# All four elements of a group turned by the DMA engines, in two halves through one free tile

## The chip, the cores and the metric

The kernel runs on one core of a Trainium2 chip. The metric is the device time of one execution in microseconds (us). Before the change the median of two runs is 2303.45 us (2301.77 and 2305.13).

The core's engines work side by side, each through its own list of instructions in order: TensorE (PE: matmuls; PEld: loading the stationary operand), VectorE (DVE), ScalarE (ACT), GpSimd (POOL) and SyncE (SP), which in this kernel issues every DMA. An instruction that must wait holds up all that stands behind it on its engine. That holds for SP too: a DMA that waits for its source holds up the DMAs listed after it.

## The reference

The input `x` holds 128 elements of 128 nodes with 512 features each, in float32. Two layers follow one another; each normalises, applies a graph operation and adds the result to its input:

```python
h = jnp.maximum(_layernorm(x, axis=-1), 0.0)
x = x + norm_adj @ (h @ W0) + b0            # layer 0, for each element
h = jnp.maximum(_layernorm(x, axis=-1), 0.0)
q, k, v = h @ Wq + bq, h @ Wk + bk, h @ Wv + bv      # 8 heads of 64
attn = softmax(q @ k.T / 8 + (1 - adj) * -1e9)
x = x + (attn @ v) @ Wo + bo                # layer 1, for each element
```

The change touches `h` of layer 1. The products with Wq, Wk and Wv contract over the features, so `h` has to lie with features on the partitions, while the normalisation leaves it with nodes on the partitions. Each 128x128 block must be transposed.

## The kernel before, in words

**Groups and blocks.** The 128 elements are worked in 32 groups of four (`GB = 4`, `NG = 32`); the elements of a group are b = 0 to 3, and b = 0, 1 are its first half, b = 2, 3 its second. An iteration t has five blocks of seven steps: W (layer 0's weight product of group t+1), Q, K and V (projections of group t), and Y (attention's output product of group t-1). Each of these products of 512 by 512 is a two-level Winograd scheme of seven products, which is why operands have extra slots of sums and differences (`combine`, lines 359 to 370). The last two parts of a block's last product are put into steps 1 and 2 of the next block (the list `tail`): TensorE writes `bank_c`, VectorE adds it to its target, and then `bank_c` is written again.

**The order.** The order of all instructions is written out by hand. `at(t, place, f, ...)` puts a function in front of a step of TensorE's dense work: "Y2" is in front of step 2 of block Y, "Y0b" after its matmuls and before its later reads. `block` (line 1012) calls them in that order, and each engine keeps to it.

**What belongs to the transposition of `h`.** In iteration t, group g = t+1 is prepared. For groups 2 to 30:

- `norm_h` (ScalarE, line 333) writes `h` of b = 0 and 1 at V1 and V2, and of b = 2 and 3 at V5 and V6.
- `split_h` (line 677) at V2b and V3: a 32-bit element is two 16-bit halves. ScalarE copies `h` of b = 0 and then b = 1 into a tile of two planes (line 682), all first halves in one plane and all second halves in the other. The tile is `att_of(g - 1, -1)`, the one attention tile of five that is free then. After the second copy SP stores the tile into `planes_h` in DRAM (line 684).
- `turn_h` (line 686) at Y0: a DMA transpose reads `planes_h` and writes eight slots of the operand tile `op_norm` (line 689).
- `transpose_h` (line 667) for b = 2 and 3 at Y1 and Y2: four TensorE transposes against the identity into a PSUM bank (line 674), and a ScalarE copy from there into `op_norm` (line 675).
- `attention_operands` (line 691) at Y5: GpSimd makes the sums and differences (lines 362 to 365 and 90), which block Q of iteration t+1 uses.

Groups 0, 1 and 31 are transposed by TensorE alone. The free tile is used again in the same iteration by `split_att` of b = 0 at Y3b (line 787): ScalarE writes the planes of the attention there, and SP stores them (line 791).

**SP's list around it.** From V3 on: the store of `planes_h` (line 684), a part of a weight reload (line 992), the DMA transpose of Y0 (line 689), weight parts at Y0, Y1 and Y3 (line 992), the store of `planes` at Y3b (line 791), a weight part at Y5, the store of a half result (line 834), two weight parts at W0, another store of `planes` at W1b, the store of the other half and the load of the first half of x of group t+2 at W3 (lines 834 and 161), the last weight part, the load of the second half at W5, and then the attention's transposes (line 794) between stores and weight parts.

**The use of x.** When x of group t+2 has landed, VectorE takes its statistics for layer 0 (line 314, first half at Q0b). On VectorE these stand between the reads of block W's tail (line 429).

Of the kernel before, what the change touches and what calls it, by code (L numbers as in the profile page):

```python
# [9 lines left out]
U16 = mybir.dt.uint16  # L10
# [16 lines left out]
A11, A12, S1, A22, S2, S3, S4 = range(7)  # L27
# [17 lines left out]
LEFT_AT = {A11: 0, A12: 4, S1: 8, A22: 12, S2: 16, S3: 20, S4: 24}  # L45
# [48 lines left out]
def kernel(  # L94
# [16 lines left out]
    nc = tc.nc  # L111
    B, N, D = x.shape
    P = 128
    H = 8
    HD = D // H
    NC = D // P
# [6 lines left out]
    dp = ctx.enter_context(tc.tile_pool(name="dp", bufs=1, space=bass.MemoryType.DRAM))  # L123
# [22 lines left out]


    planes_dram = [dp.tile([P, 2, H * P], U16, tag=f"planes_{b}", name=f"planes_{b}") for b in range(GB)]
    h_dram = dp.tile([P, 2, H * P], U16, tag="planes_h", name="planes_h")
    adj_sb, an = (att_buf[2][:, i, :] for i in range(2))  # L150
    bias_part = att_buf[4][:, 0:NC, :].rearrange("p c f -> p (c f)")
    ones = att_buf[4][:, NC, :]
# [220 lines left out]
    op_mix, op_norm, op_att = (Operands(f"op_{k}") for k in "aho")  # L373
# [303 lines left out]
    def split_h(g, b):  # L677


        h2 = hs.pop((g, b)).bitcast(U16).rearrange("n (c f z) -> n z c f", c=NC, z=2)  # L680
        planes = att_of(g - 1, -1).bitcast(U16).rearrange("n h k -> n (h k)")
        nc.scalar.copy(planes.rearrange("n (z c j f) -> n z c j f", z=2, c=NC, j=2)[:, :, :, b, :], h2)
        if b == 1:
            nc.sync.dma_start(h_dram, planes.rearrange("n (z f) -> n z f", z=2))

    def turn_h(g):
        op_h[g] = op_norm
        blocks = op_norm.t.bitcast(U16)[:, LEFT_AT[A11] : LEFT_AT[A11] + 8, :]
        nc.sync.dma_start_transpose(out=blocks, in_=h_dram.rearrange("n z f -> (n z) f"))

    def attention_operands(g):
        op_h[g].combine(nc.vector if g < 2 else nc.gpsimd, g > 0, within=nc.gpsimd)
# [42 lines left out]
    def att_of(g, b):  # L735


        return att_buf[(b - g) % (GB + 1)]
# [102 lines left out]
    def at(slot, place, f, *args):  # L841
        plan.setdefault((slot, place), []).append((f, *args))

    for t in range(-1, NG + 1):
# [3 lines left out]
        if 0 <= t - 1 < NG - 1:  # L848
            g = t - 1
# [20 lines left out]
        if t == 0:  # L870

            at(0, "Q0b", ln2, 1, 0)
            at(0, "Q1b", ln2, 1, 1)
            at(0, "K6", norm_h, 1, 0)
            at(0, "K6", norm_h, 1, 1)
            at(1, "W0", transpose_h, 1, 0)
            at(1, "W0", norm_h, 1, 2)
            at(1, "W1", transpose_h, 1, 1)
            at(1, "W1", norm_h, 1, 3)
            at(1, "W2", transpose_h, 1, 2)  # L880
            at(1, "W3", transpose_h, 1, 3)
            at(1, "W3", attention_operands, 1)
            at(2, "W6", attention_residual, 1, 0)
            at(2, "W6", attention_residual, 1, 1)
        elif 1 <= t + 1 < NG and t >= 0:
            g = t + 1
            at(t, "K0b" if g < NG - 1 else "Q0b", ln2, g, 0)
            at(t, "K3b" if g < NG - 1 else "Q3b", ln2, g, 1)
            if g == NG - 1:

                places = ("Q3", "Q4", "Q5", "Q5", "Q6", "Q6", "K1", "K2", "K2")
                steps = ((norm_h, 0), (norm_h, 1), (transpose_h, 0), (norm_h, 2), (transpose_h, 1), (norm_h, 3))
                steps += ((transpose_h, 2), (transpose_h, 3))
            else:
                places = ("V1", "V2", "V2b", "V3", "V5", "V6", "Y1", "Y2", "Y5")
                steps = ((norm_h, 0), (norm_h, 1), (split_h, 0), (split_h, 1), (norm_h, 2), (norm_h, 3))
                steps += ((transpose_h, 2), (transpose_h, 3))
                at(t, "Y0", turn_h, g)
            for place, (f, b) in zip(places, steps):
                at(t, place, f, g, b)  # L900
            at(t, places[8], attention_operands, g)
            at(t + 1, "Q3", attention_residual, g, 0)
            at(t + 1, "Q4", attention_residual, g, 1)
# [6 lines left out]
        if 2 <= t + 2 < NG:  # L910
            g = t + 2
# [3 lines left out]
            places = (("Q3", "Q5"), ("Q4", "Q6"), ("Q5b", "K1"), ("Q6", "K2"))  # L915
# [6 lines left out]
        if 0 <= t < NG:  # L922
            g = t
# [30 lines left out]
        if last:  # L954
            g = t
# [208 lines left out]
```

## Time and profile before

| | |
|---|---|
| median of the runs | 2303.45 us |
| profiled execution | 2300.24 us |
| its span | 2298.4 us |
| granted TensorE clock | 0.998 of full speed |
| busy: PE, DVE, ACT, POOL | 99%, 81%, 59%, 81% |
| time of the hardware queue's DMA packets, as a share of 16 engines | 81.2% |
| TensorE transposes of `h` (line 674) | 276, 273 ns (median) each |
| ScalarE copies from PSUM (line 675, group `op_h`) | 66, 586 ns each |
| ScalarE copies into planes (line 682) | 58, 1042 ns each |
| store of `planes_h` (line 684) | 29, 3.0 us from issue to landing (median) |
| DMA transpose of `planes_h` (line 689) | 29, 4.7 us from issue to landing (median) |

The span is the time from the first to the last instruction of the program in the profiled execution; that execution's own time is a little longer. Matmuls overlap: the durations of two that follow each other add up to more than the time they take, and start to start is the better measure. The shares are means over 2298 us, and an iteration takes some 70 us, so a share says little of the stretch in which an instruction stands; the busy table by stretches does that. The chain of waits goes back from the end of the program, at each step to what released it.

### The profile page before, as it was taken

To read this page: it belongs to the slowest core of one execution; us is meant where nothing else is said; L and a number is where in the kernel's file an instruction comes from. 1 tells how busy PE (TensorE), PEld (TensorE's weight loads), DVE (VectorE), ACT (ScalarE), POOL (GpSimd) and SP (SyncE) were. 2 spreads that over 40 slices of the span, in tenths; PEclk is the share of its full clock that TensorE was granted. 3 is DMA by queue.
4 is the path that set the end of the run, shared out by engine and by line. 5 is a ranking of instruction groups with operands and counts; after the bars stand their busy time and mean duration, and the time that the engine had idled before them with its cause. 6 is when DMAs were issued, how large, how long until landed. Compare 5 with 4: busy or idle time off the path is not lost.

```text
span 2298.4 us, 50576 instructions
## 1 busy us (share of the span) xinstructions
PE 2274.9 (99%) x18127; PEld 2131.8 (93%) x18127; DVE 1863.2 (81%) x4832; ACT 1366.8 (59%) x3553; POOL 1862.8 (81%) x1927
## 2 busy tenths in 40 slices
PE   8999999999999999999999999999999999999999
PEld 8889999999999999999999999999999999999998
DVE  6778888788888888887888888888877888888876
ACT  3555666655656556566566565566665665655654
POOL 6898888788888787888888887879877788878864
PEclk9999999999999999999999999999999999999999
DMA  6388978889887888788897788987888988789873
GB/s 200 123 260 272 270 247 257 238 251 298 240 253 235 252 269 257 257 244 246 249 304 244 242 240 248 278 258 253 241 248 248 285 251 244 241 249 289 235 230 115
DMA packets 455259, 566.46 MB, mean 246 GB/s; under 512 B 332640, under 2 KB 339936, under 8 KB 454496
## 3 DMA queue, kind: packets, MB, share of 16 engines
q1 hardware_dynamic: 455008, 563.23, 81.2%
q8 instruction: 144, 2.36, 0.4%
q14 instruction: 107, 0.88, 0.1%
HBM read 358.68 MB, written 124.26 MB: 210 GB/s over the span
## 4 chain that ended last, share of the span: by engine, by line
PE 74%; POOL 6%; DMA 6%; DVE 3%; issue 2%; ACT 2%; SPq 0%; POOLq 0%; DVEq 0%; ACTq 0%
PE bank_a L388 27%; PE bank_d L388 16%; PE bank_c L388 8%; PE bank_b L388 8%; PE pa L605 4%; DMA xt<-in_x_dram 4%; PE bank_d L750 3%; PE po L816 3%; POOL xt L337 2%; DVE xt L429 2%; PE pss L750 1%; PE bank_b L816 1%; PE bank_a L816 1%; PE bank_b L750 1%; POOL att L765 1%
## 5 line engine op out<-in xcount | busy, mean ns | idle before, releaser
L777 ACT ACTIVATE att<-att,nmx 128x128 f32<-128x128 f32 x1024 | 396.3, 391 | 0.9 <-DVE nmx L769 0.9
L388 PE MATMUL bank_a<-op_h,w 128*128 128x256 f32 x1488 | 353.3, 380 | 0.0
L785 POOL TENSOR_TENSOR att<-att,rsm 128x1024 f32<-128x1024 f32 x128 | 243.1, 1900 | 80.3 <-DVE rsm L784 79.9
L388 PEld LDWEIGHTS bank_a<-op_h,w 128*128 128x128 f32 x1488 | 270.0, 191 | 29.4
L429 DVE TENSOR_TENSOR xt<-xt,bank_d 128x512 f32<-128x512 f32 x732 | 268.8, 415 | 19.2 <-DVE xt L429 1.4
L790 ACT COPY att<-att 128x2048 uint16<-128x2048 uint16 x124 | 234.9, 1895 | 60.5 <-POOL att L785 60.5
L333 ACT ACTIVATE h<-xt,nb,rs 128x512 f32<-128x512 f32 x254 | 207.3, 817 | 69.2 <-POOL nb L322 67.4
L711 ACT ACTIVATE q<-bank_a,bqk 128x256 f32<-128x256 f32 x192 | 80.6, 471 | 265.4 <-PE bank_a L388 265.4
L320 POOL TENSOR_TENSOR rs<-ve,mhalf 128x2 f32<-128x2 f32 (+1 forms) x129 | 91.3, 708 | 180.1 <-DVE ve L319 179.7
L90 POOL TENSOR_TENSOR op_o<-op_o 128x256 f32<-128x256 f32 x297 | 210.1, 734 | 10.0
L388 PE MATMUL bank_d<-op_h,w 128*128 128x128 f32 (+1 forms) x1712 | 216.9, 278 | 0.7 <-issue 0.3
L90 POOL TENSOR_TENSOR op_a<-op_a 128x256 f32<-128x256 f32 x279 | 197.1, 730 | 14.9 <-DVE op_a L365 5.3
L388 PEld LDWEIGHTS bank_d<-op_h,w 128*128 128x128 f32 x1712 | 203.1, 192 | 5.0 <-issue 3.4
L90 POOL TENSOR_TENSOR op_h<-op_h 128x256 f32<-128x256 f32 x270 | 190.7, 731 | 13.1 <-DVE op_h L365 3.8
L777 ACT ACTIVATION_READ_ACCUMULATOR att<-att,nmx 128x1 f32 x1024 | 194.8, 190 | 0.0
L314 DVE BATCH_NORM_STATS2 st<-xt 128x6 f32<-128x512 f32 x256 | 172.9, 675 | 20.3 <-DMA xt<-in_x_dram 20.0
L388 PE MATMUL bank_a<-w,op_o 128*128 128x256 f32 x768 | 181.7, 379 | 0.0
L388 PE MATMUL bank_a<-w,op_h 128*128 128x256 f32 x744 | 179.1, 384 | 0.0
L388 PE MATMUL bank_a<-w,op_a 128*128 128x256 f32 x744 | 176.9, 381 | 0.2 <-DVE xt L439 0.2
L439 DVE TENSOR_TENSOR xt<-bank_a,xt 128x512 f32<-128x512 f32 x252 | 166.9, 684 | 11.5 <-PE bank_a L388 3.9
L757 DVE SCALAR_TENSOR_TENSOR att<-bank_d,msk 128x512 f32<-128x512 f32 x128 | 82.4, 686 | 104.7 <-PE bank_d L750 96.2
L769 DVE TENSOR_REDUCE nmx<-att 128x8 f32<-128x1024 f32 x128 | 154.9, 1210 | 0.0
(188 smaller groups left out, 5936.2 us busy)
## 6 DMA issues: line engine op xcount, KB each, us to landing
w<-wd_v SPq DMA_DIRECT2D x93, 704.0 KB, 5.6
w<-wd_o SPq DMA_DIRECT2D x93, 704.0 KB, 7.1
planes<-att SPq DMA_DIRECT2D x124, 512.0 KB, 4.5
w<-wd_q SPq DMA_DIRECT2D x90, 704.0 KB, 6.1
w<-wd SPq DMA_DIRECT2D x87, 704.0 KB, 5.6
xt<-in_x_dram SPq DMA_DIRECT2D x63, 512.0 KB, 6.5
out_dram<-xt SPq DMA_DIRECT2D x62, 512.0 KB, 4.1
planes_h<-att SPq DMA_DIRECT2D x29, 512.0 KB, 3.0
```

The costliest lines, as they stand in the source:

```text
L90: engine.tensor_tensor(twice(out), twice(x), twice(y), ALU.subtract if minus else ALU.add)
L314: nc.vector.bn_stats(self.st[:, j, :], self.src[:, j, :])
L333: nc.scalar.activation(h, src[:, j, :], AF.Relu, bias=nb[:, j : j + 1], scale=rs[:, j : j + 1])
L388: nc.tensor.matmul(out, lhsT, rhs, start=start, stop=True, skip_group_check=True)
L429: nc.vector.tensor_tensor(dst, dst, src, f)
L439: nc.vector.tensor_tensor(t, src.rearrange("p (r f) -> p r f", r=2), t, ALU.add)
L750: nc.tensor.matmul(pss[p][:, c, :], qs[g][rows, c, cols], ks[g][rows, c, cols], start=True, stop=True)
L769: nc.vector.tensor_reduce(nmx, att_of(g, b), AX.X, ALU.max, negate=True)
L777: nc.scalar.activation(att[:, h, :], att[:, h, :], AF.Exp, bias=nmx[:, h : h + 1], scale=1.0, accum_out=sm[:, h : h + 1])
L785: nc.gpsimd.tensor_tensor(att, att, rsm.unsqueeze(2).to_broadcast([P, H, P]), ALU.mult)
L790: nc.scalar.copy(planes, halves)
L816: nc.tensor.matmul(po[p * HD : (p + 1) * HD, c * P : (c + 1) * P], vs[g][:, b, h * HD : (h + 1) * HD], aT[:, p * NC + c, :], start=True, s ...
```

## The change

There are now two buffers in DRAM, `planes_h0` and `planes_h1`, one for each half of a group. `split_h` is called for all four elements: as before for b = 0 and 1 at V2b and V3, and now for b = 2 and 3 at Y0 and Y0b. Each pair goes through the same free tile, and after the second element of a pair its planes are stored into that half's buffer. `turn_h` has a second call at Y2, which turns the second half into the eight slots from S1 on, where the transposes of TensorE had been copied. For groups 2 to 30 `transpose_h` isn't called any more; groups 0, 1 and 31 are as they were. `attention_operands` stays at Y5.

```diff
-    h_dram = dp.tile([P, 2, H * P], U16, tag="planes_h", name="planes_h")
+    h_dram = [dp.tile([P, 2, H * P], U16, tag=f"planes_h{i}", name=f"planes_h{i}") for i in range(2)]
...
     def split_h(g, b):
+        half, j = divmod(b, 2)
         h2 = hs.pop((g, b)).bitcast(U16).rearrange("n (c f z) -> n z c f", c=NC, z=2)
         planes = att_of(g - 1, -1).bitcast(U16).rearrange("n h k -> n (h k)")
-        nc.scalar.copy(planes.rearrange("n (z c j f) -> n z c j f", z=2, c=NC, j=2)[:, :, :, b, :], h2)
-        if b == 1:
-            nc.sync.dma_start(h_dram, planes.rearrange("n (z f) -> n z f", z=2))
-
-    def turn_h(g):
+        nc.scalar.copy(planes.rearrange("n (z c j f) -> n z c j f", z=2, c=NC, j=2)[:, :, :, j, :], h2)
+        if j == 1:
+            nc.sync.dma_start(h_dram[half], planes.rearrange("n (z f) -> n z f", z=2))
+
+    def turn_h(g, half):
         op_h[g] = op_norm
-        blocks = op_norm.t.bitcast(U16)[:, LEFT_AT[A11] : LEFT_AT[A11] + 8, :]
-        nc.sync.dma_start_transpose(out=blocks, in_=h_dram.rearrange("n z f -> (n z) f"))
+        first = LEFT_AT[S1 if half else A11]
+        blocks = op_norm.t.bitcast(U16)[:, first : first + 8, :]
+        nc.sync.dma_start_transpose(out=blocks, in_=h_dram[half].rearrange("n z f -> (n z) f"))
...
-                places = ("V1", "V2", "V2b", "V3", "V5", "V6", "Y1", "Y2", "Y5")
+                places = ("V1", "V2", "V2b", "V3", "V5", "V6", "Y0", "Y0b", "Y5")
                 steps = ((norm_h, 0), (norm_h, 1), (split_h, 0), (split_h, 1), (norm_h, 2), (norm_h, 3))
-                steps += ((transpose_h, 2), (transpose_h, 3))
-                at(t, "Y0", turn_h, g)
+                steps += ((split_h, 2), (split_h, 3))
+                at(t, "Y0", turn_h, g, 0)
+                at(t, "Y2", turn_h, g, 1)
```

## Prediction

> **What bounds the kernel now.** I read the totals first, then the order of TensorE's instructions in one iteration, then the chain of waits, and last what the DMA engines do just before the place the chain points to. The totals and the row of DMA shares:
>
> ```profile
> span 2298.4 us, 50576 instructions
> PE 2274.9 (99%) x18127; PEld 2131.8 (93%) x18127; DVE 1863.2 (81%) x4832; ACT 1366.8 (59%) x3553; POOL 1862.8 (81%) x1927
> DMA  6388978889887888788897788987888988789873
> ```
>
> TensorE is busy 99% of the span, so removing matmuls looks like a gain one for one. But DMA stands at about eight tenths too, and an average hides where that is ten tenths. The timeline of TensorE around the transposes that go:
>
> ```profile
> 1013.34 0.60 PE L674 MATMUL pt<-ident,h 128*128 128x128 f32 x4
> 1013.78 0.61 PE L388 MATMUL bank_c<-w,op_h 128*128 128x128 f32 x4
> ...
> 1015.79 0.60 PE L674 MATMUL pt<-ident,h 128*128 128x128 f32 x4
> 1016.22 0.39 PE L388 MATMUL bank_c<-w,op_h 128*128 128x128 f32 x2
> ```
>
> From start to start, four transposes take 0.44 and 0.43 us (the durations overlap). That is 0.87 us an iteration. The 70 us iterations are not all alike, though: from the first `po` of line 816 to the next, 28 of them take between 70.06 and 71.0 us. The chain of waits of a long one shows why:
>
> ```profile
> 1731.97 0.76 DVE xt L429 x2
> 1732.73 0.02 issue
> 1732.75 0.39 SPq L834
> 1733.14 0.05 issue
> 1733.18 0.02 SPq L161
> 1733.20 0.03 issue
> 1733.23 8.99 DMA xt<-in_x_dram
> 1742.22 0.02 issue
> 1742.24 0.71 DVE st L314
> 1742.95 0.02 issue
> 1742.97 0.18 DVE mv L315
> 1743.16 0.18 DVE xt L429
> 1743.34 0.02 issue
> 1743.36 0.30 DVE xt L429
> 1743.66 0.04 issue
> 1743.70 0.49 PE bank_c L388 x2
> ```
>
> The load of the first half of group t+2 (I call it x0) lands 8.99 us after its issue. VectorE waits for it at `bn_stats` (line 314), and queued behind that, in order, is the read of `bank_c`, without which TensorE may not start the last two matmuls of block W's tail. So x0 and TensorE already race in every iteration. I take the issue of the `planes_h` store (V3) as zero of each iteration and read x0's landing and the start of those two matmuls, from the issues and landings in the trace. Over 28 iterations x0 lands at 29.9 to 31.6 us, mean 30.78, and the matmuls start at 32.39 us, or 1.48 us after the landing if that is later (31.31 gives 32.79, 31.64 gives 33.12). The excess over 32.39 sums to only 5.6 us now: the race is almost a tie. After it nothing else waits; to the next V3 it is a fixed 37.67 us.
>
> What x0 waits for is the DMA queue. The busy table by stretches of the iteration whose V3 is at 1007.08:
>
> ```profile
> 1007.00:1020.00 13.00, 13.00 (x95) 12.23 (x94) 11.72 (x30) 11.28 (x40) 11.79 (x9) 1.00 0.92 282
> 1020.00:1026.00 6.00, 6.00 (x42) 5.58 (x41) 5.63 (x16) 3.92 (x11) 5.84 (x5) 1.00 0.69 231
> 1026.00:1038.00 12.00, 12.00 (x85) 11.26 (x84) 11.45 (x31) 4.82 (x25) 10.40 (x13) 1.00 1.00 329
> ```
>
> The last two columns are the DMA share and GB/s. From V3 to 1020 the engines are 92% busy (most of the rest is the 0.94 us before the first packet), 69% from 1020 to 1026, and full from 1026 until x0 has landed. Everything put into this queue after V3 moves x0, except what fits into the free time.
>
> **The change part by part.** 29 iterations (groups 2 to 30) are touched; in 28 of them an x0 follows.
>
> Removed on TensorE: 8 transposes, 0.87 us, all of it before the race. The two matmuls could start at 31.52 instead of 32.39; all 29 together would be 25.2 us, the most this change can win.
>
> ScalarE: two PSUM copies (line 675, 586 ns) become two plane copies (line 682, 1042 ns), +0.9 us an iteration. It is busy 59% of the span, and the copies no longer wait for TensorE (51.8 us of waits at line 675 now). By its order: the last `norm_h` ends at 1012.8, both copies by 1014.7, the eight exponentials between Y1 and Y2 by 1017.8. Cost nothing; without that cover 0.9 us.
>
> SP and the DMA queue, walked from V3: first store to 1009.5, weight part, transpose and weight part of Y0 to about 1016.2. The second store is issued at 1014.7 and queues behind these, landing at about 1018.1. The weight part of Y1 follows, and it covers SP's new wait: the second DMA transpose must wait for that store. Behind it in SP's order stand the weight part of Y3 (1016.64 now), the `planes` store of Y3b (1020.37) and the weight part of Y5; the transpose's issue occupies SP for 2.57 us (median of line 689; up to 5.1 us on line 794), so they come at about 1021 to 1022. None is itself urgent: block W begins at 1024 with a weight part that landed at 1012.6. But they end before x0's predecessors may begin.
>
> The price of the added transfers: a store's 4096 byte packets take 1.53 us of 16 engines (mean of 28). A transpose's 2048 packets of 256 bytes take 3.03 us, but they overlap (the shares reach 1.3); of the 11.6 us in which the queue runs without a gap to 1019.55, the store takes 1.5, three weight parts 2.15 each and the short one 1.3 (their packets' time), which leaves 2.3 us for the transpose. So 3.8 us is added. The free time between V3+11 and V3+24 is 2.1 us in the mean. That puts x0 later by 1.7 us; the walk along the queue gives 1.5; I take **1.6 us**. Ends: 1.53+1.53-2.9 = about 0.2 (a transpose at a store's price, all free time used, the little before V3+11 too) and 1.53+3.03-1.2 = 3.4 us (no overlap, the least free time).
>
> [...]
>
> GpSimd: `attention_operands` starts at 1022.31, just when the second transpose lands (issue 1018.1 plus 4.1 to 6.7 us as on line 689, so 1022.2 to 1024.8). A delay of 0 to 2.5 us; it ends at 1034.3 now and its result is needed at 1037, with 1.2 and 0.5 us idle behind it. I take nothing; a delay beyond 2.5 us would go to TensorE.
>
> The free tile: `split_att` (Y3b) now waits until the second store has read it, 1018.1 against the 1017.8 at which ScalarE arrives, and 1018.46 now. Nothing.
>
> **The sum.** New start of the two matmuls: 30.78+1.6+1.48 = 33.86 against 31.52 without a wait, a stall of 2.34 us, 28 times 65.5. Less the 25.2 us won and the 5.6 us of stall that is there already: +34.7 us. The profiled execution took 2300.2 us (span 2298.4), 3 us under the median of 2303.45; so 2335 by that execution, and 2338 as a time to be measured.
>
> **Rivals.**
> *The gaps swallow the transfers (faster).* The mechanism is the same queue: taking the 28 landings one by one, the sum is zero where x0 comes 0.36 us later, -10 us (2293) where it isn't moved, and -20 us (2283) where it comes half a us sooner. For it: 31% free from 1020 to 1026, and nothing asks for the moved transfers at once. Against: 3.8 us into 2.1.
> *SP is blocked longer.* With a full ring a transpose's issue takes 4.6 to 5.1 us (line 794), not 2.3; the weight part of Y3, the `planes` store and the weight part of Y5 come late, and the ring runs empty behind the transpose. x0 late by 2.2 to 3.4 us: +51 to +85 us, 2354 to 2388. Against: the wait has a weight part as cover.
> *GpSimd becomes the bound*: the second transpose lands past 1025, the operands reach TensorE late in Q1; each us beyond is 29 us: 2350 to 2380.
> That the transposes aren't removed can be excluded: no call of `transpose_h` is left for these groups.
>
> **How the numbers follow.** Forecast (x0 late by 0.9 to 2.2 us, 2318 to 2354): 0.55. Gaps swallow (2283 to 2318): 0.20. SP blocked: 0.19. GpSimd: 0.06. Leaving out one in ten at each end gives 2296 to 2370. A measurement of this kernel tells some 2% from no change: slower begins at 2349.5, that is at 2.0 us; the two slow cases and the top of the forecast give 0.28. Faster by 2% would need 2257, beyond the 25 us at stake: 0.01. Within: 0.71.
>
> **What will show it.** `planes_h` store and transpose 58 times each; line 674 at 44 instead of 276. The wait of VectorE's line 314 for x0 grows from 20 to some 60 us, and TensorE's `bank_c` wait for VectorE from 5.1 us, 12 times, to 50 or 65, 28 times. DMA from 1020 to 1026 goes from 0.69 to nearly 1. x0 lands at V3+32.4, the iterations take 71 to 72 us. If x0 lands at V3+31 or sooner the forecast is wrong towards the gain; if TensorE's new idle time stands elsewhere than at `bank_c`, the mechanism is wrong.

## Result and profile after

The changed kernel takes **2358.28 us** (median of 2 runs, 2353.49 and 2363.08) against 2303.45 before: a ratio of 1.0245, 95% interval 1.0211 to 1.028 (the two medians alone give 1.0238). It is slower by 2.4%, where 2338 us (1.5%) had been forecast. The profiled execution after the change is the one of 2363.08 us, the slower of the two.

The totals on the page of the changed kernel, and its row of DMA shares:

```profile
span 2361.1 us, 50198 instructions
PE 2274.5 (96%) x17895; PEld 2125.2 (90%) x17895; DVE 1859.6 (79%) x4832; ACT 1390.0 (59%) x3553; POOL 1860.1 (79%) x1927
DMA  5388988889989899888898887988888987889883
```

Read the first engine twice. TensorE runs 232 matmuls fewer than before (17895 against 18127), the eight transposes of 29 iterations, and yet it is busy for the same 2275 us. The span is 62.7 us longer, so TensorE now stands still for 86.6 us where it stood for 23.5. So two things are to be explained: the idle time, and busy time that did not shrink.

The idle time first. These are groups from the waits of TensorE, VectorE, GpSimd and SP after the change; the columns are microseconds in total, times, and the longest. In the new kernel line 691 is the DMA transpose of `h` (689 before) and line 161 is still the load of x:

```profile
PE bank_c L388 <- DVE xt L429: 65.2, 30, 4.1
...
DVE st L314 <- DMA xt<-in_x_dram: 90.2, 30, 4.9
...
POOL op_h L362 <- DMA op_h<-planes_h: 60.5, 22, 4.7
...
SPq L161 <- DMA out_dram<-xt: 231.8, 56, 6.2
SPq L691 <- DMA planes_h<-att: 196.9, 58, 6.0
...
ACT att L792 <- DMA planes_h<-att: 60.5, 28, 3.9
```

Three of them in the kernel before:

```profile
PE bank_c L388 <- DVE xt L429: 5.1, 12, 1.3
...
DVE st L314 <- DMA xt<-in_x_dram: 20.0, 20, 3.1
...
SPq L161 <- DMA out_dram<-xt: 140.6, 28, 5.9
```

The first line is the stall that was forecast, at the place that was forecast: 5.1 us in 12 waits before, 65.2 us in 30 now. The second is what feeds it: VectorE waits for x0 (the first half of x of group t+2) 90.2 us instead of 20.0. The third is new and harmless: GpSimd waits 60 us for the second transpose, and no wait of TensorE for GpSimd's operands stands among TensorE's groups. The fourth was 140.6 us in 28 waits before, for the second half of x only. Now the first half waits too, for the store that frees its buffer. The last line is new as well: ScalarE may write the planes of the attention into the free tile (Y3b) only when the second store has read it.

The chain of waits through one iteration after the change (start, length, what), V3 being at 1034.26:

```profile
1051.86 7.17 DMA out_dram<-xt
1059.03 0.02 issue
1059.05 0.02 SPq L161
1059.06 0.03 issue
1059.09 7.31 DMA xt<-in_x_dram
1066.41 0.02 issue
1066.43 0.70 DVE st L314
...
1067.89 0.49 PE bank_c L388 x2
```

Compare its head with the chain before: there the step ahead of x0's issue was a half result that VectorE had just finished, which in turn goes back to TensorE. Here a DMA waits for a DMA, 14.5 us in a row. TensorE stands in the chain up to 1049.45, ahead of that store, and after it only at the end, as the one that is kept waiting. In all 28 iterations the two `bank_c` matmuls start 1.48 to 1.49 us after x0 has landed.

The busy table by stretches of the same iteration, cut as the one before (from V3 on; the last two columns are the DMA share and GB/s):

```profile
1034.00:1047.00 13.00, 13.00 (x94) 12.27 (x94) 12.35 (x32) 11.66 (x40) 11.75 (x10) 1.00 0.93 282
1047.00:1053.00 6.00, 6.00 (x41) 5.58 (x40) 5.67 (x14) 4.39 (x11) 2.56 (x2) 1.00 1.05 126
1053.00:1065.00 12.00, 12.00 (x85) 11.26 (x84) 10.18 (x29) 5.49 (x27) 11.36 (x13) 1.00 1.01 407
```

The middle stretch held 0.69 before and holds 1.05 now: in this iteration the free time is full and does not run empty behind a blocked SP. It moves fewer bytes, though (126 GB/s against 231): the second transpose's 2048 packets of 256 bytes stand there. In the mean of the 28 iterations the free time isn't used up: between V3+11 and V3+24, where the prediction counted 2.1 us, 1.03 us stays free.

Now the busy time that did not shrink. The same table in an iteration with a long stall, in short stretches (the column before the DMA share is the granted TensorE clock):

```profile
1136.00:1141.00 5.00, 1.65 (x15) 1.46 (x14) 0.98 (x3) 1.36 (x4) 3.74 (x3) 1.00 0.61 201
1141.00:1143.00 2.00, 1.55 (x9) 1.56 (x10) 1.90 (x7) 0.00 (x0) 0.51 (x1) 0.73 1.08 417
1143.00:1145.00 2.00, 2.00 (x7) 1.67 (x7) 1.48 (x6) 0.81 (x1) 1.90 (x4) 0.50 1.18 231
1145.00:1147.00 2.00, 2.00 (x14) 1.85 (x13) 1.93 (x6) 0.74 (x3) 1.10 (x1) 0.91 1.17 228
```

And TensorE's timeline there (start, length; in brackets the idle time before and its releaser):

```profile
1141.44 0.49 PE L388 MATMUL bank_c<-w,op_a 128*128 128x128 f32 x2 [3.79 <-DVE xt L429]
...
1143.32 2.90 PE L388 MATMUL bank_a<-op_h,w 128*128 128x256 f32 x8
...
1148.96 1.89 PE L388 MATMUL bank_a<-op_h,w 128*128 128x256 f32 x8
```

TensorE waits 3.79 us, and then its granted clock is half (0.50) for 3.41 us: eight matmuls of the same form take 2.90 us in that stretch and 1.89 us six microseconds later. In the profiled execution there are 13 such stretches in the 28 iterations, 47.8 us in all (twelve of 3.41 us, one of twice that). If half of that time is lost, it is 23.9 us, almost exactly the 24.4 us (28 times 0.87) that the removed transposes gave. That is why "busy" is the same in both pages.

The sum for the profiled execution, over the 28 iterations: stalls 67.9 - 5.1 = +62.8 us, transposes -24.4, half clock +23.9: +62.3, and the span grew by 62.7.

### The profile page after: what moved, and what is told of

Its sections match the earlier page's. It is cut to its first block, busy times and chain, and to the rows that moved or that the text cites. A ratio compares the mean times of both kernels' runs of the same rounds, so it can differ in the third digit from the quotient of the medians.

```text
span 2361.1 us, 50198 instructions
## 1 busy us (share of the span) xinstructions
PE 2274.5 (96%) x17895; PEld 2125.2 (90%) x17895; DVE 1859.6 (79%) x4832; ACT 1390.0 (59%) x3553; POOL 1860.1 (79%) x1927
## 4 chain that ended last, share of the span: by engine, by line
PE 69%; DMA 18%; DVE 5%; issue 1%; ACT 0%; SPq 0%; POOL 0%; DVEq 0%
PE bank_a L388 25%; PE bank_d L388 15%; DMA xt<-in_x_dram 9%; DMA out_dram<-xt 9%; PE bank_b L388 8%; PE bank_c L388 7%; PE pa L605 4%; PE bank_d L752 3%; PE po L818 2%; DVE xt L439 2%; DVE xt L429 2%; PE pss L752 1%; PE bank_b L818 1%; PE bank_a L818 1%; PE bank_b L752 1%; DVE st L314 1%
## 5 line engine op out<-in xcount | busy, mean ns | idle before, releaser
L388 PE MATMUL bank_a<-op_h,w 128*128 128x256 f32 x1488 | 369.4, 393 | 0.0
L388 PEld LDWEIGHTS bank_a<-op_h,w 128*128 128x128 f32 x1488 | 280.9, 199 | 33.3
L792 ACT COPY att<-att 128x2048 uint16<-128x2048 uint16 x124 | 235.3, 1898 | 88.7 <-DMA planes_h<-att 60.5
L314 DVE BATCH_NORM_STATS2 st<-xt 128x6 f32<-128x512 f32 x256 | 173.3, 677 | 90.2 <-DMA xt<-in_x_dram 90.2
```

The costliest lines, as they stand in the source:

```text
L314: nc.vector.bn_stats(self.st[:, j, :], self.src[:, j, :])
L388: nc.tensor.matmul(out, lhsT, rhs, start=start, stop=True, skip_group_check=True)
L792: nc.scalar.copy(planes, halves)
```

## Experiments

I measured three numbers of each iteration: x0's landing, counted from V3; the stall ahead of the `bank_c` pair; and TensorE's time at half clock (28 iterations of the profiled execution). The stall counts from when the pair could have started, one matmul's step after the matmul before it; that is 0.17 us more for each wait than the idle time in the profile, which begins at that matmul's modelled end. The times are medians of all runs, the other columns are of one execution, which can lie some us to either side of the median.

| kernel | time, us | ratio to before, 95% | x0 lands, mean | stalls, us | half clock, us |
|---|---|---|---|---|---|
| before | 2303.45 | | 30.78 | 5.1 | 0 |
| after | 2358.28 | 1.0211 to 1.028 | 32.53 | 67.9 | 47.8 |
| e1_pe_kept | 2360.85 | 1.0253 to 1.0288 | 32.74 | 50.7 | 27.3 |
| e2_no_second_dma | 2276.05 | 0.9881 to 0.991 | 29.89 | 4.2 | 0 |
| e5_store_only | 2310.44 | 1.0023 to 1.0056 | 31.13 | 29.3 | 3.4 |
| e6_turn_only | 2296.15 | 0.9968 to 0.9996 | 30.61 | 16.4 | 3.4 |
| e7_turn_y3b | 2351.65 | 1.02 to 1.0235 | 32.19 | 58.4 | 17.1 |
| e4_weights_after_x | 2306.18 | 1.0012 to 1.0035 | 30.61 | 22.7 | 13.7 |
| e10_spin | 2342.55 | 1.0166 to 1.0202 | 32.19 | 26.2 | 10.2 |
| e3_stats_at_q3 | 2287.10 | 0.993 to 0.996 | 32.02 | 0 | 3.4 |
| e9_stats_and_bias | 2284.40 | 0.9903 to 0.9946 | 32.53 | 0 | 0 |
| b9_stats_and_bias | 2300.20 | 0.9983 to 1.0002 | 30.69 | 0 | 0 |
| e11_stats_bias_mix | 2288.46 | 0.994 to 0.9964 | 32.15 | 0 | 0 |

The kernel before took 2300.4 to 2301.7 us (medians of 11 to 25 runs) on the chips of these experiments; the ratios of the experiments are to those. My **theory**: the added transfers make x0 late, and x0 sets the pace. The **rivals**: SP, blocked by the second transpose's issue and its wait, holds up the loads; GpSimd gets the operands late; or the pause of TensorE itself costs more than its length.

### The matmul saving, put back: e1_pe_kept

Eight transposes per iteration that nobody reads are put back on TensorE where the removed ones stood.

```diff
+    def idle_transposes():
+        pt = small_bank("pt_idle")
+        for c in range(NC):
+            nc.tensor.transpose(pt[:, c * P : (c + 1) * P], ident, ident)
...
+                at(t, "Y1", idle_transposes)
+                at(t, "Y2", idle_transposes)
```

> The changed kernel with the eight TensorE transposes put back (of the identity, into a bank nobody reads), so that TensorE saves nothing and the DMA engines still carry the second pair of transfers. If the landing of x0 sets the end of each iteration, it still lands at V3+32.5 us and the last pair of bank_c matmuls still starts 1.48 us later; only the stall before them shrinks, by 0.87 us each time (from 68 us to some 45). Long stalls become rarer, so fewer stretches of half clock (48 us in the changed kernel, some 25 to 30 here): 2345 to 2358 us against 2358. If instead TensorE's work sets the time and the saving is being had, putting it back costs 25 us: 2380 us or more.

2360.85 us, a little above the range expected, and no different from the changed kernel's 2353.49 to 2363.08. TensorE's wait for x0 falls from 65.2 to 48.4 us, as if the transposes were done inside it:

```profile
PE bank_c L388 <- DVE xt L429: 48.4, 30, 4.0
```

So while x0 decides, the work removed from TensorE is worth nothing. TensorE is no longer the bound.

### The transfers, left out: e2_no_second_dma

The planes of the second half are still copied, but neither stored nor turned.

```diff
-        if j == 1:
+        if b == 1:
...
-                at(t, "Y2", turn_h, g, 1)
```

> The changed kernel without the second store and without the second DMA transpose of each group (the split copies on ScalarE stay); the second half of the operands is then not renewed, so that part of the computation is left out. If the added transfers are the cause, x0 lands at V3+30.8 us again, the bank_c pair starts at V3+32.3 in the mean, the stalls sum to some 20 us with none above 1.7 us and no half clock: 2285 to 2296 us. If ScalarE's longer copies, or the removal itself, did the harm, the time stays above 2303 us.

2276.05 us: 24.4 us below the kernel before it ran beside (2300.43), the full price of the transposes (28 times 0.87). TensorE's totals and its wait in this kernel:

```profile
PE 2248.8 (99%) x17895; PEld 2107.2 (93%) x17895; DVE 1857.9 (82%) x4832; ACT 1386.7 (61%) x3553; POOL 1860.5 (82%) x1927
...
PE bank_c L388 <- DVE xt L429: 4.3, 9, 1.3
```

With the same 17895 matmuls TensorE is busy 2248.8 us here and 2274.5 in the changed kernel. The result is better than the 2285 to 2296 that I expected, and the miss is instructive: I had taken x0's landing as fixed from V3, but it came at 29.89 instead of 30.78, 0.89 sooner. Its issue goes back to TensorE, and TensorE got there 0.87 us sooner; x0 is issued at V3+21.85 instead of 22.67. ScalarE's longer copies are still there and do no harm. Everything bad about the change is thus in the added transfers: 82 us lie between this kernel and the changed one, and x0 is 2.64 us later there.

### The two transfers apart: e5_store_only and e6_turn_only

e5 keeps the second store and drops the second transpose; e6 stores only the first half and turns its planes twice.

```diff
 e5_store_only
-                at(t, "Y2", turn_h, g, 1)
 e6_turn_only
-        if j == 1:
+        if b == 1:
...
-        nc.sync.dma_start_transpose(out=blocks, in_=h_dram[half].rearrange("n z f -> (n z) f"))
+        nc.sync.dma_start_transpose(out=blocks, in_=h_dram[0].rearrange("n z f -> (n z) f"))
```

> The changed kernel with the second store of each group but without the second DMA transpose (the second half of the operands isn't renewed, that part of the computation is left out). Without both transfers x0 landed at V3+29.89 in the mean and the time was 2276 us; with both at V3+32.53. If each transfer pays for the time of its packets in one queue, the store's 1.53 of 4.56 us is a share of some 0.9 us: x0 at about V3+30.8, the bank_c pair at 32.3, 2285 to 2300 us. If the price is SP's wait of the second transpose for the second store, which isn't there any more, x0 stays within 0.4 us of 29.9 and the time within 5 us of 2276.

> The changed kernel with the second DMA transpose but without the second store: it reads the first half's buffer again, so that the second half of the operands gets the first half's values (that part of the computation is left out) and the transpose needn't wait for a store. If each transfer pays for the time of its packets, this is the larger share, 1.7 us: x0 at about V3+31.6, the pair at 33.1, 2310 to 2330 us. If the price is SP's wait for the store, x0 stays within 0.5 us of 29.9 and the time within 8 us of 2276.

From e2's 29.89, the store alone moves x0 by 1.24 us (31.13) and the transpose alone by 0.72 (30.61). I had it the other way round: by the transfers' packets, the transpose should have been the dearer one. What differs is how much free time of the queue a transfer fills. By the packets' times (means of 28 iterations, V3+11 to V3+24) 1.55 us are free in e2, 1.25 in e5, 0.44 in e6 and 1.03 in the changed kernel. So the store alone fills 0.30 us, the transpose alone 1.11, the pair 0.52; delay and filled time together are 1.54, 1.83 and 3.16 us (1.13, 1.58 and 2.87 when the stretch runs from V3+2 to x0's landing). That is an estimate of the time each takes in the queue, and by it the transpose is the dearer one after all. The store leaves free time because it also makes ScalarE wait for the free tile (line 792 for `planes_h`, 55.6 us in 27 waits in e5, none in e6): the store of `planes` at Y3b is issued at V3+14.76 instead of e2's 12.50. e6 took 2296.15 us where 2310 to 2330 was expected; e5 took 2310.44, just above its range. TensorE's wait in e5 and in e6:

```profile
PE bank_c L388 <- DVE xt L429: 27.7, 25, 2.8
...
PE bank_c L388 <- DVE xt L429: 15.2, 18, 2.3
```

Alone they add up to 1.96 us, together they cost 2.64. The missing 0.68 us needs both. One thing that only the pair has is the wait of the second transpose for its own store: SP's waits of that kind (line 691 for `planes_h`) are 70.7 us in e5, 73.4 in e6 and 196.9 in the changed kernel. By the estimate above it is free time that stays unfilled: the two alone fill 1.41 us, the pair 0.52. SP's wait can be what keeps it open. That SP is held by the issue of a transpose is in e6's price already: the second one's issue takes 5.67 us there in the mean, the weight part of Y3 goes out at V3+12.86 instead of e2's 8.73, and x0 comes only 0.72 us late. Whether the wait for the store is the cause of the 0.68 us is what e7 asks.

### The second transpose issued later: e7_turn_y3b

```diff
-                at(t, "Y2", turn_h, g, 1)
+                at(t, "Y3b", turn_h, g, 1)
```

> The changed kernel with the second DMA transpose at Y3b instead of Y2, so that the short weight part of Y3 stands before it in SP's list and is no longer held up by its wait for the second store. The DMA work is the same. If the price lies in SP's order (the store alone moved x0 by 1.2 us, the transpose alone by 0.7, both together by 2.6), x0 lands some 0.5 us sooner, V3+32.0, and the time is 2335 to 2348 us. If it lies in the sum of the transfers, x0 stays at V3+32.5 and the time at 2352 to 2364 us.

2351.65 us, between the two expectations. The waits of SP for the store shrink only a little, and so does x0's delay (32.19 against 32.53):

```profile
SPq L691 <- DMA planes_h<-att: 166.4, 58, 5.5
```

The free time is filled here, to 0.28 us, and yet x0 gains no more. The order on SP can be part of the 0.68 us, but this run does not settle how much.

### Another transfer behind x0: e4_weights_after_x

If x0 is late because the queue ahead of it is full, moving any transfer behind x0 must help. One of the two weight parts of W0 is moved to W3, where it follows x0.

```diff
-            "Y": ((t, "Y5"), (t + 1, "W0"), (t + 1, "W0"), (t + 1, "W3" if t + 1 < NG - 1 else "Q5")),
+            "Y": ((t, "Y5"), (t + 1, "W3" if t + 1 < NG - 1 else "W0"), (t + 1, "W0"), (t + 1, "W3" if t + 1 < NG - 1 else "Q5")),
```

> The changed kernel with one of the two Wq weight parts of W0 (704 KB, first used at Q4) issued behind the load of x0 instead of before it. Nothing is left out and the DMA work is the same; only the order in SP's list differs. If the length of the queue ahead of x0 is the cause, x0 lands some 1.7 to 2.2 us sooner, V3+30.5 in the mean, the stalls fall to 15 to 25 us, no half clock: 2285 to 2300 us. If x0 is late because SP is held up (behind the second transpose, or for the stores that free x's buffers), the landing hardly moves and the time stays above 2340 us.

x0 comes at 30.61, 1.92 us sooner than in the changed kernel and as expected, and 52 of the 55 us lost are back. But 2306.18 us misses the expected range, because the landings now scatter (28.66 to 33.64) and TensorE pays for each late one and gains nothing from an early one:

```profile
PE bank_c L388 <- DVE xt L429: 21.9, 18, 3.3
```

So x0's landing goes with what stands ahead of it in the DMA queue. By the issues in the traces (means of 28 iterations) x0 is issued at V3+24.66 here and at 24.92 in the changed kernel, when the store that frees its buffer has landed, but then takes 5.95 us here and 7.62 there. That store itself is issued in the changed kernel only 0.37 us later than in e2 (17.24 against 16.87) and lands 4.28 us later (24.85 against 20.57): that time is spent in the queue, not in SP's list. e4 takes other work out of the queue; that the added transfers are what lengthens it is shown by e2, e5 and e6. How much the late issues of the transfers between them add is not separated.

### TensorE kept busy through the pause: e10_spin

Is the half clock brought on by the length of TensorE's pause? Then work that nobody needs, put into the pause, should make the kernel faster. Twelve transposes of the identity are put in front of step Q2 of the groups in the middle.

```diff
+            if 1 < t < NG - 2:
+                for _ in range(3):
+                    at(t, "Q2", idle_transposes)
```

> The changed kernel with 12 additional TensorE transposes of the identity, 1.3 us of work that nobody reads, just before the pair of bank_c matmuls that waits (Q2). TensorE's wait there becomes shorter by what the additional work takes, its end doesn't move. In the changed kernel 13 waits of 2.4 us or more were each followed by 3.4 us at half clock, 48 us in all, which by the length of the matmuls cost 24 us. If the length of TensorE's pause brings the half clock, at most 5 such stretches are left, and more work makes the kernel faster: 2338 to 2350 us. If the half clock has another cause, it stays as it is: 2356 to 2364 us.

2342.55 us, 16 us less than the changed kernel, with 336 matmuls more. The pause is cut into work and a shorter wait:

```profile
PE 2293.0 (98%) x18231; PEld 2149.0 (92%) x18231; DVE 1858.7 (80%) x4832; ACT 1390.7 (60%) x3553; POOL 1862.5 (80%) x1927
...
PE bank_c L388 <- DVE xt L429: 25.4, 20, 3.5
```

Half clock falls from 47.8 to 10.2 us, worth 18.8 us at half speed, while x0 still lands at 32.19. So the stall and the half clock are two costs: the stall comes from the queue, the half clock from the stall.

### The statistics of x taken later: e3_stats_at_q3, e9_stats_and_bias, b9_stats_and_bias, e11_stats_bias_mix

If the wait hurts only because `bank_c`'s read is queued behind it on VectorE, then the statistics should stand later on VectorE. e3 moves both halves from Q0b and Q1b to Q3, and what follows from them by a step.

```diff
-            at(t, "Q0b", ln1, g, 0, (0,), ())
-            at(t, "Q1b", ln1, g, 0, (1,), (0, 1))
+            at(t, "Q3", ln1, g, 0)
-            places = (("Q3", "Q5"), ("Q4", "Q6"), ("Q5b", "K1"), ("Q6", "K2"))
+            places = (("Q4", "Q6"), ("Q5", "K1"), ("Q6", "K2"), ("K1", "K3"))
-            at(t, "K2" if t > 0 else "V1b", gcn_operands, g)
+            at(t, "K3" if t > 0 else "V1b", gcn_operands, g)
```

> The changed kernel with the statistics of x0 moved on VectorE from Q0b and Q1b to Q3, behind the reads of block W's tail and of block Q's first products; the normalisations and products that use them, and the operands made from these, come one place later. x0 lands as late as in the changed kernel, but the reads of bank_c no longer stand behind it. If the queueing on VectorE is what carries the late landing to TensorE, the bank_c stall of 68 us goes to a few us, the clock stays full and the saved transposes are won: 2275 to 2295 us. If the late DMAs hurt TensorE in other places too (operands, weights, the second half of x), those waits appear instead and it stays above 2320 us.

2287.10 us: faster than the kernel before (0.9945, 0.993 to 0.996), with x0 as late as 32.02 and no stall at the pair at all. Of the 82 us between e2 and the changed kernel 71 are gone without a transfer being touched. What is left of the way to e2's 2276 is another wait, TensorE for ScalarE's normalisation, some 0.6 us in each iteration (in e2 it was 7.0 us in 4):

```profile
PE pa L605 <- ACT h L333: 20.1, 30, 4.3
PE bank_c L388 <- DVE xt L429: 3.3, 3, 1.6
```

To shorten this I moved GpSimd's bias additions out of the way (e9), and made the same two moves in the kernel before (b9), to see whether the moves alone are what is faster.

```diff
-            at(t + 1, "Q3", attention_residual, g, 0)
-            at(t + 1, "Q4", attention_residual, g, 1)
+            at(t + 1, "Q6", attention_residual, g, 0)
+            at(t + 1, "K0", attention_residual, g, 1)
```

> The changed kernel with the statistics of x0 at Q3 as before (2287 us), and the additions of the output bias on GpSimd moved from Q3 and Q4 to Q6 and K0. In the run with the statistics alone TensorE waited some 0.5 us in each iteration for h, whose scale stood on GpSimd behind such an addition of 2.4 us. If that is the remaining wait, it goes and the time falls by 10 to 14 us, to 2272 to 2280 us, where the kernel without the second pair of transfers stands (2276). If the wait comes from x0's own landing or from VectorE, it stays at 2284 to 2290 us.

> The kernel before, with the same two moves (statistics of x0 at Q3, bias additions at Q6 and K0) and with its TensorE transposes of the second half as they were. If the moves only take away the race with x0, they win the 5 us of stalls that are there: 2293 to 2299 us. The 87 hundredths of a us by 29 iterations, 25 us, between this and the changed kernel with the same moves would then be what the DMA transposes are worth. If the moves are themselves the gain and the change has none, this kernel is as fast as the changed one with them.

e9 takes 2284.40 us, not clearly less than e3; the bias additions were not the remaining wait, which stays:

```profile
PE pa L605 <- ACT h L333: 16.6, 30, 4.4
```

b9 takes 2300.20 us, a ratio of 0.9992 (0.9983 to 1.0002) to the kernel before, where 2293 to 2299 had been expected: the moves alone bring nothing, though the stalls of 5 us are gone. With them the change itself is worth 2300.2 - 2284.4 = 15.8 us, 0.7%. Of the kernels that compute everything e9 has the lowest median, 0.9925 of the kernel before.

e11 moves the first mixed operand of e9 from Q6 to Q6b, so that the awaited normalisation comes sooner.

```diff
-            places = (("Q4", "Q6"), ("Q5", "K1"), ("Q6", "K2"), ("K1", "K3"))
+            places = (("Q4", "Q6b"), ("Q5", "K1"), ("Q6", "K2"), ("K1", "K3"))
```

> The changed kernel with the statistics of x0 at Q3 and the bias additions at Q6 and K0 (2284 us), and the first of the four products that use the statistics after step Q6's matmuls instead of before them. In the run without this, TensorE waited there 0.4 us in each iteration for h. If that wait is the last one in the loop, it goes: 2270 to 2277 us, where the kernel without the second pair of transfers stands (2276). If x0's landing still shows in another place, it stays at 2280 us or more.

A miss, 2288.46 us. The wait for the normalisation is gone (2.9 us in 2), and one of the same size has come on VectorE's side:

```profile
PE bank_b L388 <- DVE q L429: 18.3, 29, 1.8
```

The last 8 us between e9 and e2 I did not find a place for.

## Why the prediction was right or wrong

**The bound and the place: right.** x0's race with TensorE, the `bank_c` pair behind VectorE's line 314, and the DMA queue before it carried the case. The stretch ahead of x0's queue fills to 1.05 in the iteration shown, the stall stands at `bank_c` in every iteration, and e3 removes it by moving VectorE's wait alone. That ScalarE's longer copies cost nothing holds too: it is busy 23 us more (1390.0 against 1366.8), no wait of TensorE comes of it, and e2 wins the full price with these copies in place.

**The stall: right in size.** 65.5 us were forecast, 67.9 measured; x0 was forecast at 32.4 and landed at 32.53.

**But by luck: two errors cancel.** "x0 later by 1.6" was counted from 30.78, as though x0's landing were fixed from V3. e2 shows that without the transfers it moves up with TensorE, to 29.89. The transfers then cost 2.64 us, not 1.6. The chain quoted in the prediction held the hint: x0's issue stands behind a store, the store behind VectorE's sum, and that behind TensorE. The prices of the rival that the gaps swallow the transfers fall with it: if the transfers cost x0 nothing, the time is not 2293 but 2276, the whole 24 us won.

**The split of the 3.8 us: wrong.** A store of 1.53 and a transpose of 2.3 less 2.1 of free time gave 1.7, taken as 1.6. The runs gave 1.24 for the store alone, 0.72 for the transpose alone and 0.68 more for both together. The mis-sized term is the free time: 1.03 us of it stays free, so the pair could not hide 2.1 us in it. By the estimate under e5 and e6 the pair takes 2.9 to 3.2 us in the queue, less than 3.8. The walk along the queue was too early as well: it had the second store land at V3+11.0, and it lands at 12.81 in the mean. The free tile, put at nothing, makes ScalarE wait 60.5 us in 28 waits; what x0 pays for that is not separated. The low ends, x0 late by 0.2 us and by the 0.9 us at which the forecast's range begins, were the author's estimate with a transpose at a store's price, 1.53 us. No run shows that price: the estimates from these runs are 1.6 to 1.8 us for the transpose alone against 1.1 to 1.5 for the store.

**The term that is missing: the half clock.** This is where the sum failed. The forecast's sum, 65.5 - 25.2 - 5.6 = +34.7 us, has no price for what a pause does to TensorE afterwards. Measured, that is +23.9 us in the profiled execution, and it is most of the 28 us between the +34.7 forecast and the +62.7 that came; the rest is 2.9 us of stall and the small differences of the other terms. (By the medians the change costs 54.8 us, 20 more than forecast.) e10 shows that it hangs on the pause. It can be part of the 9.6 us by which the two runs of the changed kernel differ: their mean granted clocks are 0.988 and 0.990.

**The rivals.** *The gaps swallow the transfers*: no; the added work fills 0.52 us of e2's 1.55, and the rest of it delays x0. *SP is blocked longer* had the right time, 2354 to 2388, and by that alone one could take it for the cause. A part of it came: the weight part of Y3, the `planes` store and the weight part of Y5 are issued at V3+15.28, 15.90 and 16.40 instead of 9.56, 13.29 and 13.69, by SP's wait for the store more than by the issue of the second transpose, which takes 2.29 us in the mean. The queue runs empty behind it only in part (share 1.05 in the table above, 1.03 us free in the mean against 0.44 in e6), and the store that x0 waits for is issued hardly later. e6, in which SP is held by an issue of 5.67 us, has x0 only 0.72 us late in all. What SP's wait for the store adds, by keeping free time unfilled, has its place in the 0.68 us that the pair costs more than its parts; how much of that it is stays open. *GpSimd becomes the bound*: its wait came (60.5 us in 22 waits, 3.54 us long ahead of the operand of this iteration) and nobody waited for it.

**What was to show it.** All of the list came but for sizes: 58 stores and transposes, 44 transposes left on line 674, VectorE's wait at 90 instead of 60 us, TensorE's at 65.2 in 30 waits, iterations of 72.6 us in the mean where 71 to 72 was said. The list had no line for the clock.

## What to carry to other kernels

Work taken off the busiest engine is worth its time only until the next thing in line is late: look for the closest race (here x0 and TensorE, tied within a microsecond) and ask on which side of it the replaced work lands. When a transfer comes late, first move the instruction that waits for it behind those that do not need it (e3); that brought back nearly all, and made the change a small gain. A stall of TensorE can be dearer than its length (in the five kernels counted below 18 of 21 pauses of 3 us or more were, and none of up to 2.16 us): read the granted clock in the stretches after it, and price both.

## What I had not expected of the hardware

**The half clock after short pauses.** The stretches at half clock are 3.413 us long (one is twice that), and their starts differ by multiples of 3.413 us (995.16 to 1141.93 is 43 of them): by these starts they lie on one raster of that step. A pause is counted here like the stalls in the table. Over the five kernels with several of them (the changed one, e1, e4, e7, e10; 140 iterations) a pause of up to 2.16 us was never followed by one (0 of 95), one between 2.17 and 2.99 us in 12 of 24 cases, and one of 3.0 us or more in 18 of 21. Among the other kernels, the one stretch in e6 (at 201.27 us) follows a pause of 1.64 us of idle time and a shorter one close behind it, so the length of one pause does not tell all. The shortest pause that one followed lasted 2.17 us, less than the 3.413 us of a stretch, and a pause of 3.54 us passed without.

**A transpose's packets say little of the delay it makes.** With 3.03 us of engine time against 1.53 for the store, it moved the load behind it by 0.72 us against 1.24 (e6 and e5). Some of that is the free time that it filled; with it the estimates are 1.6 to 1.8 us and 1.1 to 1.5, still well under the packets' 3.03 for the transpose.
